# Correlation matmuls joined by four on 32-row groups, and the last head pair's sums on 32 columns, in an eight-image attention and correlation kernel

## The chip, the core and the metric

The kernel runs on one core of a Trainium2 chip. Its engines are TensorE (PE in the profile, its weight loads PEld), VectorE (DVE), ScalarE (ACT), GpSimd (POOL) and SyncE (SP), which issues most of the DMAs. Each engine has a queue of its own and takes its instructions in their order. The metric is the device time of one launch in microseconds (us), lower is better.

## The reference

Input: eight images of 768 channels by 1024 pixels (32 x 32), float32. Two layers follow each other, each behind a group norm and added to its input. Layer 0 is an attention with 12 heads of 64 whose scores are the product of two vectors; layer 1 puts 28 correlations of the image with itself, shifted by up to three pixels, beside the 768 channels and multiplies all 796 by a weight.

```python
# layer 0
qkv = x_flat @ W_qkv.T                                  # 12 heads of 64
var_v = jnp.var(v, axis=-1, ddof=1, keepdims=True)
var_k = jnp.var(k, axis=-1, ddof=1, keepdims=True)
scores = var_v @ jnp.swapaxes(var_k, -2, -1) * scale
out = jax.nn.softmax(scores, axis=-1) @ v
out = out.reshape(B, N, C) @ W_proj.T + b_proj
...
# layer 1
feat_n = feature / jnp.maximum(norm, EPS)
corr = jnp.stack([jnp.sum(feat_pad[:, :, r:h + r, cc:w + cc] * feat_n, axis=1) for r, cc in _offsets()], axis=1)
x = jnp.concatenate([feature, corr], axis=1)            # 768 + 28 channels
out = jnp.einsum('bchw,oc->bohw', x, conv_w) + conv_b[None, :, None, None]
...
x = x + layer0(_gn(x))
x = x + layer1(_gn(x))
```

`_offsets()` are the two diagonals, the middle column and the middle row of a 7 by 7 window.

## The kernel before

**Products.** The large matrix products (keys and values, the projection, the 768-channel part of layer 1, called conv here) go by a fast scheme with 7 products for 8 blocks. The products are numbered 1 to 7; those of one output group g are added up in PSUM tiles named `x`, `y` and `z` (`BANK`, two tiles of x and two of y, which z uses too). `PAIR` and `SINGLE` give the order of (g, p) for the projection and the conv: groups 0 and 1 in turn, then group 2. A product of these two is 12 matmul records in the profile, one for each of three blocks, two column halves and the two passes of float32. `Banks.begin` issues one, `Banks.close` sets when VectorE takes the finished tile (`Wide.take`), and the next product into that tile waits for it. The weights come as tiles `wt`, one for each product, loaded by SP in `t_stream.keys` order as the tiles come free. Sums of operands that the scheme needs (t1, t2, third, t4) are made by VectorE; `t1o` to `t4o` belong to the projection, `t1f` to `t4f` to the conv.

**Attention.** Since the scores of a head are an outer product, `ex` is one ACT instruction with a scale for each row. Two heads make a pair `hp` of six; a pair has eight steps `t`. In each step ACT makes two `ex` tiles and TensorE adds `ex` by `v` into `av` (`Pair.products`, L763, eight records a step). For pairs 3, 4 and 5 (in image 0 for pair 0 too) the denominators are the column sums of `ex`: VectorE adds the eight steps into `acc_5_0` and `acc_5_1` (one tile for each head), and TensorE multiplies them by ones. For the other pairs ACT sums over rows (L748, `junk`) and the inverses go to their places by way of DRAM (`di`, `rd`). `Pair.sum_up` (L797) does it with 32 columns of ones, all four blocks of head and half side by side in one PSUM tile `den`, whose rows go by DRAM to a narrow tile, get their reciprocal there, and come back as `rd`. `Pair.sum_up_last` (L847), for the last pair, uses 64 columns of ones and two PSUM tiles, so that the sums stand on the partitions that need them, and VectorE takes four reciprocals of 128 x 256 into `acc_5_0`. `Pair.finish` multiplies `v` (the pair's output) by the inverses.

**Correlation.** `Corr.gram` (L1101) makes the products of each pixel with those around it, `diagonals` picks the shifted ones, `scale` multiplies by the norm and turns them (`ct`, L340, after `dn`); `gather` (L1174 on, eleven DMAs on SP) puts 40 rows into `cs` (`u`) and `v`, and VectorE multiplies them. 40 channels for 28 correlations: 18 offsets ahead, the same 18 behind, and 4 rows for the middle, with zero weights for those that no correlation uses. `cs` holds three variants of the tokens (first half, second half, difference); rows 0 to 39 are copied to rows 64 to 103.

**Joins.** For images 0 to 6 the correlation part is added inside the conv's own PSUM tiles: 12 products of a conv (p of 2, 3, 7, 4) are left open, and as soon as two are held, `Wide.join` (L1008) adds a matmul with `cs` and `wcorr_sb` to each, the first on rows 0 to 39, the second on rows 64 to 103. The last image's correlation has products and PSUM tiles of its own (L1280).

**Order.** Nothing is scheduled by the tool chain: the program issues instructions in the order in which a model of time (`Clock`) reaches them. `clock.now` follows TensorE, `clock.act` and `clock.dve` follow the two others, `after(us, job)` and `after_dve(us, job)` put a job at a due time, and each job's instructions go to the engine queues in that order. On the chip only the queues and the semaphores count. For each image b + 1 the loop makes keys and values, then `work_off` issues the attention's steps whenever they can run, with the correlation and conv of image b in between. When the rest of that other work is at most `TAIL` us, it is kept back for the gaps and the time after the attention. Then `project(b + 1)` runs the projection, which takes all six pairs' outputs: pairs 0 to 2 in the products of `v` and `t1o`, `t2o` and the later sums with pair 5's too. The projection's results come to `f` (preloaded with the image, `f<-in_x_dram`), on to DRAM as `x1d` and back as the accumulator `x` of the next conv.

At the start TensorE runs `WARM` matmuls on a unit matrix (`warm`, L390) while the first image loads; the group norm's two small products (`pma`, `pva`) follow.

Of the kernel before, what the change touches and what calls it, by code (L numbers as in the profile page):

```python
# [6 lines left out]
F32 = mybir.dt.float32  # L7
# [31 lines left out]
NCH = 2 * NA + 4  # L39
# [11 lines left out]
TAIL = 14.0  # L51
# [3 lines left out]
WARM = 36  # L55
# [13 lines left out]
ORDER = (1, 5, 6, 3, 7, 4, 2)  # L69
OPENING = PAIR[:2] + PAIR[-2:] + PAIR[2:-2]  # L70

# [87 lines left out]
def two_layers(ctx, tc, x, wkv, wproj, bproj, wconv, wcorr, bconv, out):  # L159
# [147 lines left out]
    class TStream:  # L307
        def __init__(self):
            self.keys = []
            for b in range(NB + 1):  # L310
                for kind in ["c"] * (b > 0) + ["p"] * (b < NB):
                    some = PAIR[:-2] if b == NB - 1 and kind == "c" else PAIR
                    self.keys += [(kind, g, p) for g, p in some + SINGLE]
            at = len(self.keys) - len(PAIR + SINGLE)
            self.keys[at:at] = [("c", g, p) for g, p in PAIR[-2:]]
            self.loaded, self.tiles = 0, []
# [25 lines left out]
    class Banks:  # L342
# [11 lines left out]
        def begin(self, g, p, width, pairs, stop=True, between=None):  # L354
            bank = BANK[p]
            of = "x" if bank == "x" else "y"
# [31 lines left out]
    warm = smp.tile([P, 512], F32, tag="sm", name="warm")  # L388
    for n in range(WARM):
        nc.tensor.matmul(warm[:, 0:P], lhsT=ident, rhs=ident, start=True, stop=True)  # L390
# [53 lines left out]
    def load_corr_weights():  # L444
# [5 lines left out]
        for line, step in enumerate(STEP):  # L450
            for j in (1, 2, 3):
                n, k = AHEAD_OF.index(step * j), 3 * line + j - 1
                nc.sync.dma_start(out=wcorr_sb[n : n + 1, :, :], in_=wcorr[k : k + 1, :, :])
                nc.sync.dma_start(out=wcorr_sb[NA + n : NA + n + 1, :, :], in_=wcorr[12 + k : 13 + k, :, :])
        nc.sync.dma_start(out=wcorr_sb[2 * NA : NCH, :, :], in_=wcorr[24:28, :, :])
        nc.sync.dma_start(out=wcorr_sb[HD : HD + NCH, :, :], in_=wcorr_sb[0:NCH, :, :])

# [10 lines left out]
    class Norm:  # L468
# [7 lines left out]
        def means(self):  # L476
            name, mv = self.name, self.mv
            pm = small(f"pm{name}")
            halves(pm[:, 0:1], group_m, mv[:, 0:1])
            self.mean = st.tile([P, 1], F32, tag="mean", bufs=2, name=f"mean{name}")  # L480
# [6 lines left out]
        def spreads(self):  # L487
            name = self.name
            pv = small(f"pv{name}")
            halves(pv[:, 0:1], group_m, self.e)  # L490
            ve = st.tile([P, 1], F32, tag="ve", name=f"ve{name}")
# [216 lines left out]
    class Pair:  # L708
# [80 lines left out]

        def sum_up(self):  # L790
# [3 lines left out]
            for e in range(2):  # L794
                for hf in range(2):
                    at = 2 * e + hf
                    nc.tensor.matmul(  # L797
                        den[at * 32 : (at + 1) * 32, :], lhsT=ones[:, 0:32], rhs=self.acc[e][:, hf * HF : (hf + 1) * HF],
                        start=True, stop=True,
                    )  # L800
# [30 lines left out]
        def load_inverses(self, rows):  # L831
# [5 lines left out]
            self.rd_at = clock.now + (14.0 if (self.b, self.hp) == (1, HP // 2 - 1) else 6.0)  # L837
            self.try_finish()

        def sum_up_last(self):  # L840

            dens = []
            for hf in range(2):
                at = slice(hf * HF, (hf + 1) * HF)
                den = other([P, HF], f"den{self.b}_{self.hp}_{hf}")
                for e in range(2):
                    nc.tensor.matmul(  # L847
                        den[e * HD : (e + 1) * HD, :], lhsT=ones, rhs=self.acc[e][:, at], start=True, stop=True
                    )
                dens.append(den)  # L850
            self.rd = self.acc[0]

            def invert(n):

                q = HF // 2
                vector.reciprocal(self.rd[:, n * q : (n + 1) * q], dens[n // 2][:, n % 2 * q : (n % 2 + 1) * q])
                if n < 3:
                    later.after_dve(1.5 if self.b else 0.0, lambda: invert(n + 1))
                else:
                    self.rd_at = clock.dve  # L860
                    self.try_finish()
# [674 lines left out]
```

## Time and profile before

| what | us |
|---|---|
| runs | 2640.43, 2641.02, 2641.0 |
| median of the runs | 2641.0 |
| profiled execution, its own time | 2640.4 |
| its span, first to last instruction | 2638.7 |
| TensorE busy | 2610.0 |
| VectorE busy | 1604.3 |
| ScalarE busy | 1367.3 |
| GpSimd busy | 413.6 |

The mean granted clock of TensorE is 0.998 of full speed. The DMA queues are busy for some 52% of sixteen engines' time. The span of 2638.7 us lies inside the execution's own time of 2640.4 us; what is left is before the first and after the last instruction.

An image takes some 324 us, most of it one steady pattern that returns in images 2 to 7; image 0 (keys and values of two images, no conv beside) and image 1 differ. In a timeline a line gives the start, the duration from the first start to the modelled last end, the engine, the line of the program, the operation and how many records it stands for; in brackets is idle time just before it and who ended it. Matmuls are pipelined, so the next start tells better than start plus duration when a group is done.

### The profile page before, as it was taken

The page shows a single profiled execution, that of the slowest core. Times are in us where ns is not written, and L with a number is a line of the kernel's source. Part 1 is how long each engine was busy: PE and PEld are TensorE (multiplying, and loading weights), DVE is VectorE, ACT ScalarE, POOL GpSimd, SP SyncE. Part 2 cuts the span into 40 slices and gives each one's busy share as a digit, 9 for nine tenths or more (in the row PEclk, how much of TensorE's full clock was granted, in tenths as well). Part 3 has the DMA queues.
Part 4 walks back from the last instruction along what each step waited for, and adds up shares of the span by engine and source line. Part 5 has one row for each costly group of instructions (what it writes and reads, how often), then busy time and mean ns, then how long its engine had stood idle before and what let it go on. Part 6 is the DMA issues. An engine that isn't in the chain of part 4 may idle for free.

```text
span 2638.7 us, 40466 instructions
## 1 busy us (share of the span) xinstructions
PE 2610.0 (99%) x14766; PEld 1318.2 (50%) x14766; DVE 1604.3 (61%) x4110; ACT 1367.3 (52%) x1841; POOL 413.6 (16%) x444
## 2 busy tenths in 40 slices
PE   9999999999999999999999999999999999999999
PEld 4654566334763347633476334553357433575333
DVE  5858735685447853478534885357853587535864
ACT  1498078711598116980179701897018960199500
POOL 4320130003300033000430003300133001320000
PEclk9999999999999999999999999999999999999999
DMA  7774455455553545626556265562655626545333
GB/s 285 291 247 147 144 198 158 137 182 159 188 187 113 201 153 180 198 95 214 155 172 196 87 220 158 171 205 81 221 172 154 196 84 237 169 137 164 96 117 101
DMA packets 323392, 446.65 MB, mean 169 GB/s; under 512 B 59458, under 2 KB 245170, under 8 KB 323194
## 3 DMA queue, kind: packets, MB, share of 16 engines
q1 hardware_dynamic: 321962, 441.32, 52.0%
q8 instruction: 117, 1.92, 0.3%
q10 hardware_dynamic: 1232, 2.75, 0.3%
q14 instruction: 81, 0.66, 0.1%
HBM read 377.49 MB, written 64.40 MB: 167 GB/s over the span
## 4 chain that ended last, share of the span: by engine, by line
PE 89%; DMA 3%; ACT 3%; DVE 2%; issue 1%; SPq 1%; POOL 1%; DVEq 0%; ACTq 0%; POOLq 0%
PE x L337 35%; PE av L763 22%; PE y L337 17%; PE z L337 9%; PE gr L1101 3%; ACT ex L738 1%; ACT junk L748 1%; DMA x<-x1d 1%; DMA v<-rows 1%; DMA bc<-vdr 1%; PE x L1008 1%; PE den L797 1%; PE y L1008 1%; PE z L1008 1%; DVE acc L153 1%
## 5 line engine op out<-in xcount | busy, mean ns | idle before, releaser
L738 ACT ACTIVATE ex<-bc,nk 128x1024 f32<-128x1024 f32 x768 | 828.2, 1138 | 418.7 <-DMA bc<-vdr 202.6
L763 PE MATMUL av<-ex,v 128*64 128x512 f32 x3072 | 700.2, 596 | 3.4 <-ACT ex L738 3.2
L763 PEld LDWEIGHTS av<-ex,v 128*64 128x64 f32 x3072 | 316.6, 137 | 339.0 <-issue 210.5
L748 ACT ACTIVATE junk<-bk,vm 128x1024 bf16<-128x1024 f32 x368 | 420.5, 1143 | 25.3 <-DMA bk<-kdr 15.5
L153 DVE TENSOR_TENSOR acc<-acc,ex 128x1024 f32<-128x1024 f32 x300 | 344.3, 1209 | 0.0
L215 ACT COPY kp<-x 128x384 f32<-128x384 f32 x28 | 13.4, 477 | 562.1 <-PE x L337 553.4
L337 PE MATMUL y<-kv,s 128*64 128x384 f32 x1488 | 269.4, 487 | 0.0
L337 PE MATMUL x<-kv,xn 128*64 128x384 f32 x1512 | 264.3, 489 | 1.6 <-DVE xn L153 1.6
L337 PE MATMUL x<-kv,s 128*64 128x384 f32 x1488 | 258.2, 486 | 0.0
L337 PEld LDWEIGHTS x<-kv,xn 128*64 128x64 f32 x1512 | 145.3, 138 | 101.1 <-issue 80.5
L337 PEld LDWEIGHTS x<-kv,s 128*64 128x64 f32 x1488 | 145.2, 137 | 91.2 <-issue 67.6
L337 PEld LDWEIGHTS y<-kv,s 128*64 128x64 f32 x1488 | 140.7, 137 | 87.1 <-issue 69.2
L494 POOL TENSOR_TENSOR rstda<-vea,neghalf 128x1 f32<-128x1 f32 x8 | 4.8, 595 | 964.4 <-DVE vea L153 964.4
L1086 POOL TENSOR_TENSOR turn<-f,ones 128x384 f32<-128x384 f32 x112 | 110.9, 1010 | 248.3 <-PE gr L1101 167.6
L337 PE MATMUL z<-kv,xn 128*64 128x384 f32 x768 | 135.1, 486 | 0.0
L337 PE MATMUL x<-v,wt 128*64 128x512 f32 x576 | 131.1, 594 | 0.0
L337 PE MATMUL x<-f,wt 128*64 128x512 f32 x504 | 120.1, 594 | 0.0
L153 DVE TENSOR_TENSOR v<-y,v 128x128 f32<-128x128 f32 x180 | 40.9, 282 | 127.3 <-PE y L337 127.3
L600 POOL TENSOR_TENSOR s<-xn 128x384 f32<-128x384 f32 x64 | 66.8, 1052 | 287.2 <-PE x L337 199.0
L153 DVE BATCH_NORM_STATS2 vbn<-v 128x6 f32<-128x64 f32 x720 | 101.6, 209 | 0.0
L337 PEld LDWEIGHTS z<-kv,xn 128*64 128x64 f32 x768 | 76.4, 137 | 45.9 <-issue 34.3
L1101 PEld LDWEIGHTS gr<-f,turn 128*64 128x64 f32 x1344 | 88.3, 137 | 13.2 <-issue 5.2
(192 smaller groups left out, 3006.5 us busy)
## 6 DMA issues: line engine op xcount, KB each, us to landing
kv<-kvs SPq DMA_DIRECT2D x124, 576.0 KB
kv<-in_wkv_dram SPq DMA_DIRECT2D x95, 576.0 KB
bc<-vdr SPq DMA_DIRECT2D x96, 512.0 KB
f<-in_x_dram SPq DMA_DIRECT2D x48, 512.0 KB
bk<-kdr SPq DMA_DIRECT2D x46, 512.0 KB
x1d<-f SPq DMA_DIRECT2D x42, 512.0 KB
x<-x1d SPq DMA_DIRECT2D x42, 512.0 KB
out_dram<-x SPq DMA_DIRECT2D x82, 256.0 KB
```

Source lines behind the costliest of these rows:

```text
L153: return getattr(self.engine, name)(*args, **kw)
L215: nc.scalar.copy(to, at)
L337: nc.tensor.matmul(out[at], lhsT=lhsT[:, at], rhs=rhs, start=start, stop=stop, **kw)
L494: nc.gpsimd.tensor_tensor(self.rstd, ve, neghalf[:, 0:1], ALU.pow)
L600: nc.gpsimd.tensor_tensor(self.sums[g][:, 0], a[g][2], a[g][3], ALU.add)
L738: nc.scalar.activation(ex, self.bc[e], AF.Exp, scale=self.kv.nk[self.half][:, h, t : t + 1])
L748: nc.scalar.activation(junk, self.bk[e], AF.Exp, scale=self.kv.m2[self.half][:, h, t : t + 1], accum_out=self.sums[:, e, t : t + 1],)
L763: nc.tensor.matmul(self.av[e * HD : (e + 1) * HD, hf, :], lhsT=self.vt[:, t, e, :], rhs=exs[e][:, hf * HF : (hf + 1) * HF], start=t == 0, ...
L797: nc.tensor.matmul(den[at * 32 : (at + 1) * 32, :], lhsT=ones[:, 0:32], rhs=self.acc[e][:, hf * HF : (hf + 1) * HF], start=True, stop=True,)
L1008: nc.tensor.matmul(t, lhsT=wcorr_sb[at, i, :], rhs=cs[at, tokens, :], start=False, stop=True, skip_group_check=True)
L1086: nc.gpsimd.tensor_tensor(to[:, :, side], half, windows(ones, ones.ap[0], (0, J), (HW, 4), (1, HW)), ALU.mult)
L1101: nc.tensor.matmul(ps[side * HD : (side + 1) * HD, :n].rearrange("p (y x) -> p y x", x=WIDE), lhsT=block[:, j, side, :], rhs=image[:, 4 * ...
```

## The change

Five edits, all in the order and form of work; what is computed stays the same.

1. *Channels.* The offsets are listed as four runs of three (`PICKED`), so 12 + 12 + 4 = 28 channels are gathered instead of 40, by 14 DMAs instead of 11. `wcorr_sb` and `cs` are copied to rows 32, 64 and 96 (three copies of 28 rows, before one of 40).
2. *Joins by four.* For the conv of images 0 to 5, a new order (`QUADS`) holds four products, joins them by four matmuls on rows 0, 32, 64 and 96, does that twice, and joins the last four by twos. One product, (0, 2), stands in a tile of the small PSUM pool (`apart`). Image 6 keeps six joins of two, at rows 0 and 32. Per conv: 2 joins of four and 2 of two, before 6 of two.
3. *Last pair's sums.* `sum_up_last` uses the 32-column products of `sum_up` (now `ones_products`), one PSUM tile, two reciprocals of 128 x 256 into `acc_5_1`, and then eight DMAs on SP (32 rows x 512, 64 KB each) which copy each block of rows twice into the 64 partitions of `acc_5_0` that need it. Its reciprocals are due 1.7 us after the products (before 1.2), the copies 0.5 us after the second one.
4. *Less held.* `TAIL` goes from 14 to 11, so that in the order written out av_5's eight steps follow each other in images 2 to 7, with one product with its join between them and `den_5`; before, one product stood between the two halves of av_5. VectorE's order changes with it: in images 2 to 7 the takes of two conv tiles (`x<-z`, `x<-x`) now stand ahead of the reciprocals, and the multiplication of pair 4 (`v*rd`) behind them. `rd_at` of the other pairs goes from 6 to 8 us.
5. *Start and image 0.* 42 warm matmuls instead of 36, in the `av` tile; 6 more behind `pma` and 12 behind `pva` (`BRIDGE`). In image 0 `ct` is issued 5.0 us after its operands' due time instead of 0.7, which puts `ct_0` behind two more steps of av and a `gr`.

```diff
-NCH = 2 * NA + 4
+PICKED = ((1, 1), (31, 1), (62, 2), (93, 3))
+CHANNELS = [first + apart * n for first, apart in PICKED for n in range(3)]
+NS = len(CHANNELS)
+NCH = 2 * NS + 4
...
-TAIL = 14.0
+TAIL = 11.0
...
-WARM = 36
+WARM, BRIDGE = 42, (6, 12)
...
+QUADS = PAIR[:10] + ((0, 2),) + PAIR[10:12] + ((1, 2), (2, 5), (2, 1)) + SINGLE[2:]
+FOUR = P // 4
...
+def conv_order(b):
+    return QUADS if b < NB - 2 else (PAIR[:-2] if b == NB - 2 else PAIR) + SINGLE
...
-        def begin(self, g, p, width, pairs, stop=True, between=None):
+        def begin(self, g, p, width, pairs, stop=True, between=None, apart=False):
             bank = BANK[p]
+            if apart:
+                t = other([P, width], f"{bank}{g}")
+                for k, (lhsT, rhs) in enumerate(pairs):
+                    halves(t, lhsT, rhs, start=k == 0, stop=False, skip_group_check=True)
+                return ("apart", g), t
...
-    warm = smp.tile([P, 512], F32, tag="sm", name="warm")
-    for n in range(WARM):
-        nc.tensor.matmul(warm[:, 0:P], lhsT=ident, rhs=ident, start=True, stop=True)
+    warm = avp.tile([P, 512], F32, tag="av", name="warm")
+    def keep_warm(count):
+        for n in range(count):
+            nc.tensor.matmul(warm[:, 0:P], lhsT=ident, rhs=ident, start=True, stop=True)
+    keep_warm(WARM)
...
-        nc.sync.dma_start(out=wcorr_sb[HD : HD + NCH, :, :], in_=wcorr_sb[0:NCH, :, :])
+        for n in range(1, 4):
+            nc.sync.dma_start(out=wcorr_sb[n * FOUR : n * FOUR + NCH, :, :], in_=wcorr_sb[0:NCH, :, :])
...
             halves(pm[:, 0:1], group_m, mv[:, 0:1])
+            if name == "a0":
+                keep_warm(BRIDGE[0])
...
             halves(pv[:, 0:1], group_m, self.e)
+            if name == "a0":
+                keep_warm(BRIDGE[1])
...
+        def ones_products(self, den):
+            for at in range(4):
+                e, hf = divmod(at, 2)
+                nc.tensor.matmul(
+                    den[at * 32 : (at + 1) * 32, :], lhsT=ones[:, 0:32], rhs=self.acc[e][:, hf * HF : (hf + 1) * HF],
+                    start=True, stop=True,
+                )
...
-            self.rd_at = clock.now + (14.0 if (self.b, self.hp) == (1, HP // 2 - 1) else 6.0)
+            self.rd_at = clock.now + (14.0 if (self.b, self.hp) == (1, HP // 2 - 1) else 8.0)
...
         def sum_up_last(self):
-            dens = []
-            for hf in range(2):
-                at = slice(hf * HF, (hf + 1) * HF)
-                den = other([P, HF], f"den{self.b}_{self.hp}_{hf}")
-                for e in range(2):
-                    nc.tensor.matmul(
-                        den[e * HD : (e + 1) * HD, :], lhsT=ones, rhs=self.acc[e][:, at], start=True, stop=True
-                    )
-                dens.append(den)
-            self.rd = self.acc[0]
+            den = other([P, HF], f"den{self.b}_{self.hp}")
+            self.ones_products(den)
+            self.rd, rc = self.acc[0], self.acc[1][:, 0:HF]
+            q = HF // 2
             def invert(n):
-                q = HF // 2
-                vector.reciprocal(self.rd[:, n * q : (n + 1) * q], dens[n // 2][:, n % 2 * q : (n % 2 + 1) * q])
-                if n < 3:
-                    later.after_dve(1.5 if self.b else 0.0, lambda: invert(n + 1))
-                else:
-                    self.rd_at = clock.dve
-                    self.try_finish()
-            later.after(1.2 if self.b else 0.0, lambda: invert(0))
+                vector.reciprocal(rc[:, n * q : (n + 1) * q], den[:, n * q : (n + 1) * q])
+                later.after_dve(0.5, spread if n else lambda: invert(1))
+            def spread():
+                for at in range(4):
+                    e, hf = divmod(at, 2)
+                    to = self.rd[e * HD : (e + 1) * HD, hf * HF : (hf + 1) * HF]
+                    rows = rc[at * 32 : (at + 1) * 32, :]
+                    for half in range(2):
+                        nc.sync.dma_start(out=to[half * 32 : (half + 1) * 32, :], in_=rows)
+                self.rd_at = clock.now + 5.0
+                self.try_finish()
+            later.after(1.7 if self.b else 1.0, lambda: invert(0))
...
-                self.held.append((*banks.begin(g, p, HF, pairs, stop=False, between=between), taken, *more))
-                if len(self.held) == 2:
+                apart = (g, p) == (0, 2) and self.joined[:1] == [4]
+                self.held.append((*banks.begin(g, p, HF, pairs, stop=False, between=between, apart=apart), taken, *more))
+                if len(self.held) == (self.joined[0] if self.joined else 2):
+                    self.joined = self.joined[1:]
                     self.join()
...
             for n, (slot, t, taken, i, tokens) in enumerate(self.held):
-                at = slice(n * HD, (n + 1) * HD)
+                at = slice(n * FOUR, n * FOUR + NCH)
...
-                later.after_dve(0.7, lambda: to_dram(dn))
+                later.after_dve(0.7 if b else 5.0, lambda: to_dram(dn))
...
-            nc.sync.dma_start(out=u[0:NA, :], in_=r[2:NROW, PAD : PAD + N])
-            nc.sync.dma_start(out=v[NA:NCH, :], in_=windows(r[0:1, PAD:], (0, NA + 4), (1, N)))
...
+            for n, (first, apart) in enumerate(PICKED):
+                k, row = 3 * n, 2 + AHEAD_OF.index(first)
+                nc.sync.dma_start(out=u[k : k + 3, :], in_=windows(r[row : row + 1, PAD:], (apart * ROW, 3), (1, N)))
+                nc.sync.dma_start(out=v[k : k + 3, :], in_=windows(r[0:1, PAD + first :], (apart, 3), (1, N)))
...
-                nc.sync.dma_start(out=cs[HD : HD + NCH, :, :], in_=cs[0:NCH, :, :])
+                for n in range(1, 4):
+                    nc.sync.dma_start(out=cs[n * FOUR : n * FOUR + NCH, :, :], in_=cs[0:NCH, :, :])
...
+            self.wide.joined = [4, 4] if self.b < NB - 2 else []
```

## The prediction

> **What bounds the kernel now.** I read the busy times first. TensorE (PE) works 2610.0 of 2638.7 us; DVE and ACT have 39% and 48% of the span idle. So a microsecond counts only if it leaves TensorE's own queue of work or one of the few gaps in it. The list of what TensorE waited for gives the gaps; its timeline around the change prices each product.
>
> ```profile
> PE 2610.0 (99%) x14766; PEld 1318.2 (50%) x14766; DVE 1604.3 (61%) x4110; ACT 1367.3 (52%) x1841; POOL 413.6 (16%) x444
> ```
> ```profile
> PE x L337 <- DVE x L153: 4.6, 6, 0.9
> PE ct L340 <- DVE dn L153: 3.3, 1, 3.3
> ...
> PE ptv L340 <- DVE vm L153: 2.3, 3, 1.2
> ```
> (total, how often, longest). The timeline of TensorE in image 2 (start, duration, name; the next start, not start plus duration, tells when work is done):
> ```profile
> 800.18 2.74 PE L337 MATMUL y<-f,wt 128*64 128x512 f32 x12
> 802.86 0.69 PE L1008 MATMUL x<-cs,wcorr_sb 64*128 64x512 f32 x1
> 802.86 0.69 PE L1008 MATMUL y<-cs,wcorr_sb 64*128 64x512 f32 x1
> 803.39 0.59 PE L1008 MATMUL x<-cs,wcorr_sb 64*128 64x512 f32 x1
> 803.40 0.59 PE L1008 MATMUL y<-cs,wcorr_sb 64*128 64x512 f32 x1
> 803.91 7.09 PE L763 MATMUL av<-ex,v 128*64 128x512 f32 x32
> ...
> 850.61 1.06 PE L797 MATMUL den<-acc,ones 128*32 128x512 f32 x8
> 851.61 7.09 PE L763 MATMUL av<-ex,v 128*64 128x512 f32 x32
> ...
> 874.27 1.94 PE L847 MATMUL den<-acc,ones 128*64 128x512 f32 x8
> 876.04 2.74 PE L337 MATMUL y<-f,wt 128*64 128x512 f32 x12
> 879.51 2.79 PE L337 MATMUL x<-t4f,wt 128*64 128x512 f32 x12 [0.72 <-DVE x L153]
> ```
> A product of 12 records takes 2.575 us (24 in 893.65 to 898.80). The two correlation matmuls of a join run in pairs on two row groups, 0.53 us a pair, 1.05 in all; with the changes of form before and after (802.755 by the product's rate, 803.91 plus 0.05 that the next av loses) a join costs 1.2.
>
> **The sum, part by part** (us, minus is a gain).
>
> *Joins.* Images 0 to 5 go from six joins of two to two of four and two of two: 12 fewer. If four row groups run together as two do, a four costs no more than a two: -14.4. I add 0.05 for each four's two further starts: **-13.8**. If they ran two by two, a four would take 1.15 + 1.05 = 2.2 and 12 x (2.4 - 2.2) = -2.4 is left. I take the first: the eight records of L797 are four 32-column matmuls and take 1.00 in all, so this array does run four at once in the other direction, and the rows above show two. The four sums stand in four different PSUM tiles. The Trainium skill, "TensorE: Matmul & The Clock Gate", Part 3, Measured speedup, speaks for less: it gives 3.07 times for four row tiles at 512 columns; with a lone matmul as two records of 0.43 us (2.575 / 12, times the two column halves that run together), that estimate puts four at 4 x 0.86 / 3.07 = 1.12, and the part at -13.6. No row here shows four row groups.
>
> *Sums of the last pair.* 64 columns took 1.77 (874.27 to 876.04), 32 columns 1.00: -0.77 in images 2 to 7, -0.57 in image 1, where 545.03 to 546.75 stands less the 1.15 of a den with its change of form: **-5.2**. Both are rows, so the bounds are narrow (-4 to -5.4).
>
> *The wait before x<-t4f.* DVE did one reciprocal (875.43, 1.76) and v*rd (877.10, 1.16) before it freed the x bank at 878.77. In the new order both evacuations stand ahead of the reciprocals. By starts the loss was 879.51 - 878.62 = 0.9, with the weight load 0.95: six times, **-5.7** (0 to -5.7).
>
> *av_5 in one piece.* The product that stood between its halves gave ACT 2.6 us to get ahead with ex. Image 0 had the halves together: 63 records from 246.62 and the last until 261.19, 14.5 against 13.74 for two normal halves. I take +0.8 in images 2 to 7: **+4.8**; ends 0 and +1.4 each (ACT's mean ex of 1138 ns followed by hand over sixteen).
>
> *Reciprocals and the spread.* Four of 1.68 become two, ending 4.9 after the start of den_5 (T0). But eight DMAs must now copy the rows to their partitions, and on SP they stand behind a wt load that waits for x<-t4f to end (T0 + 1.0 + 2 x 2.58 = T0 + 6.2). SP issues small copies at 0.28 each (four den<-ds in 1.13), so they go from T0 + 6.7 to T0 + 9, land at about T0 + 12 (2.1 from di at 814.13 to the dependent rd at 816.26, more for 64 KB), and f<-in_x_dram behind them leaves at T0 + 9.8 instead of coming at 882.97. It lands 5.0 later (887.96 in DVE's timeline), at T0 + 14.8; then f<-x (0.7), v_5 times the inverse (1.2) and the first t2o (0.6): T0 + 17.5. TensorE wants t2o after den, y, x, a join of two and 48 records of v and t1o: 1.0 + 5.15 + 1.2 + 10.3 = T0 + 17.65. It meets with next to nothing over; I charge +0.3 in images 1 to 7: **+2.1** (0 to +3 each).
> ```profile
> 882.97 0.56 SPq L1336 DMA_DIRECT2D f<-in_x_dram  x1
> ```
> ```profile
> 887.96 0.75 DVE L153 SCALAR_TENSOR_TENSOR f<-x,bproj_sb,f 128x512 f32<-128x512 f32 x1 [2.23 <-DMA f<-in_x_dram]
> ```
>
> *Image 0's t2o* waited 1.62 at 288.74; the spread there stands behind a wt that waits for the first t1o product: **+1.5** (0 to +4).
>
> *ct in image 0.* Its 3.3 wait for dn goes, as some 4 us of other work (av, gr) now stands ahead of ct: it runs at about 395.7 as today, so nothing after it is later: **-3.3** (0 if dn slips with it).
>
> *Channels and gather.* 28 rows instead of 40 change no matmul's length: 512 columns move either way. But the gather is 14 DMAs instead of 11, on SP ahead of x<-x1d, and that load is late today:
> ```profile
> 760.90 0.26 SPq L1185 DMA_DIRECT2D v<-rows  x1
> 761.20 0.29 SPq L1186 DMA_DIRECT2D cs<-rows  x1
> 761.59 0.40 SPq L292 DMA_DIRECT2D kv<-in_wkv_dram  x1
> 762.10 0.42 SPq L1214 DMA_DIRECT2D x<-x1d  x1
> ```
> ```profile
> 766.85 0.75 DVE L153 SCALAR_TENSOR_TENSOR x<-x,bconv_sb,x 128x512 f32<-128x512 f32 x1 [3.94 <-DMA x<-x1d]
> ```
> DVE waits for x1d, vm follows, and ptv on TensorE follows vm at once (vm from 769.02, 0.24; ptv at 769.32). Three more issues at 0.39 each (760.41 to 761.59) make x1d 1.17 late. In images 2 to 6 ptv has 0 to 0.3 to spare, in image 7 1.3: 5 x 1.17 less 0.3 = **+5.5** (0 if the late load catches up, +15 if SP waits for one more landing, about 2 us as at 757.94 to 759.93). The two further cs<-cs copies delay nothing that TensorE needs: 20 us lie between 775.82 and the first join at 796.50.
>
> *Start.* After 72 warm records TensorE idles from 12.55 to 16.87 but for pma and pva, and the first 24 real records take 5.79 instead of 3.87, at a granted clock of 0.50 (the third number from the right in the table of stretches):
> ```profile
> 18.00:19.00 1.00, 1.00 (x4) 0.24 (x2) 1.00 (x3) 1.00 (x2) 0.30 (x1) 0.50 1.10 410
> 19.00:20.00 1.00, 1.00 (x6) 0.49 (x4) 1.00 (x2) 1.00 (x3) 1.00 (x1) 0.50 0.11 40
> ```
> The 18 new warm matmuls fill these gaps. If that keeps the clock, 1.9 is won and some 0.6 lost to the mean and spread steps queued behind them: **-1.3** (-1.6 to +0.5).
>
> The sum: -13.8 - 5.2 - 5.7 + 4.8 + 2.1 + 1.5 - 3.3 + 5.5 - 1.3 = **-15.4**. The profiled execution took 2640.4, so 2625.0; the median of the runs, 2641.0, stands 0.6 above it: **2625.6**. All terms at their lower ends give -30; all at their upper ends, joins still four at once, +28.
>
> **Rivals.** (1) *Four row groups run two by two.* For it: only two are seen together. Against: L797. Then -2.4 for -13.8: 2625.6 + 11.4 = 2637.0. (2) *Waits on the middle way take the room*: ptv 2 us late in five images (+10 for +5.5) and av_5 at its upper end (+8.4 for +4.8): 2625.6 + 8.1 = 2633.7. For it: DVE already waits 2.4 to 5.0 us for x1d. Against: SP's later waits are for loads long on their way. (3) *Slower: the spread.* The eight copies and f behind them, on one SP queue, beside xn and wt loads, arrive so late that TensorE waits before x<-t2o in images 1 to 7. The gain is gone from (15.4 + 2.1) / 7 = 2.5 us each, that is if f<-x starts later than T0 + 17.5 instead of T0 + 14.8; at 5 us it is 2625.6 + 7 x 4.7 = 2658.5. For it: the chain reaches t2o with 0.15 to spare, and every step of it is a DMA. Against: a wait of 2.5 needs the copies to take half as long again as the rows say. (4) *No change*: the gains are all cover for something else, 2641. Against: joins and dens are pure work of a 99% busy engine.
>
> **Chances.** Forecast 0.68, (1) 0.10, (2) 0.10, (3) 0.09, (4) 0.03. A measurement of this kernel tells about 0.2% (5.3 us) from no change, so faster means under 2635.7: the forecast, (2) and a little of (1), 0.79; the same, most of (1) and (4), 0.11; slower 0.10. The range, 2612 to 2641, takes in rivals (1) and (2) and leaves out (3) and the lowest corner.
>
> **What would show it.** Four L1035 records with starts within 0.1 us and a whole four-way join near 1.1 (right) or 2 (rival 1). den of the last pair at 1.00. No wait of x<-t4f for DVE x. A wait of av for ACT ex near 0.8 in images 2 to 7. The waits of x<-t2o for DVE t2o and of ptv for DVE vm: 2 and about 8 in total if I am right, over 17 for t2o under rival 3. Clock 1.00 from 17 us on. I am wrong if one of the waits I charge by hand is twice its price, or if the joins take their old time.

## The result, and the profile after

The changed kernel is slower: 2667.9 us median (2664.2 to 2671.1, five runs) against 2641.0 for the kernel before (2640.4 to 2646.2), a ratio of 1.0095 with a 95% interval of 1.0080 to 1.0109. The forecast was 2625.6, with 2612 to 2641 as its range. The profiled execution took 2671.1 us (span 2669.4), 30.8 more than that of before.

TensorE is busy for 2612.1 us, against 2610.0 before, so its work has not grown by 30 us. The page's first line of the changed kernel:

```profile
PE 2612.1 (98%) x14814; PEld 1349.3 (51%) x14814; DVE 1575.2 (59%) x4094; ACT 1366.4 (51%) x1841; POOL 414.5 (16%) x444
```

The list of what TensorE waited for in the changed kernel (total, times, longest) has new or longer entries at the top (ptv for vm stood at 2.3 before, t2o at 1.6):

```profile
PE ptv L349 <- DVE vm L163: 17.3, 5, 4.2
PE x L346 <- DVE t2o L163: 15.6, 7, 6.5
PE x L346 <- DVE x L163: 6.6, 1, 6.6
PE it L349 <- DVE invs L163: 3.3, 1, 3.3
```

All entries of such a list add up to 53.2 us, against 23.8 before. That is 29.4 more. Second, the granted clock: I added up, over all stretches of 1 us, what was missing to full clock. It is 6.1 us before and 23.3 after (0.9 and 1.1 of it behind the last instruction). Losses come in portions of 1.71 us, which is half of some 3.4 us at a clock of 0.50: three such portions before, thirteen after. All but one of the thirteen stand at the new or longer waits; the one at 484 us has its like before, at 478. The table of stretches around the ptv of image 2 in the changed kernel (the third number from the right is the clock; TensorE's busy time comes first after the length):

```profile
782.00:784.00 2.00, 0.69 (x4) 0.00 (x0) 0.00 (x0) 1.97 (x5) 0.00 (x0) 1.00 1.07 401
784.00:786.00 2.00, 0.00 (x0) 0.00 (x0) 1.47 (x6) 2.00 (x3) 0.00 (x0) 0.79 1.04 421
786.00:788.00 2.00, 1.09 (x5) 0.85 (x7) 1.97 (x8) 1.97 (x3) 0.43 (x1) 0.50 1.01 410
788.00:790.00 2.00, 2.00 (x8) 1.04 (x6) 2.00 (x5) 2.00 (x4) 0.00 (x0) 0.50 0.47 193
790.00:792.00 2.00, 2.00 (x7) 1.06 (x5) 2.00 (x10) 1.97 (x4) 0.00 (x0) 0.50 0.05 12
792.00:794.00 2.00, 2.00 (x12) 1.27 (x10) 1.34 (x2) 2.00 (x4) 0.00 (x0) 1.00 0.72 260
```

TensorE stands still for 4.2 us until 786.9, and then works at half clock until 792: 8 and 7 matmul records in two stretches of 2 us, where the next one, at full clock, has 12. Waits (+29.4) and clock (+17.2) make 46.6; the execution grew by 30.8, so some 16 us of work did go, as the change meant; the slower clock hides that in the busy time. (A portion may lie partly in a wait, so this is a bound rather than a sum.)

**The pieces that went as meant.** TensorE's timeline in image 2 of the changed kernel, first a join of four, then the end of the image:

```profile
818.91 2.90 PE L346 MATMUL y<-f,wt 128*64 128x512 f32 x12
821.74 0.69 PE L1035 MATMUL y<-cs,wcorr_sb 28*128 28x512 f32 x1
821.75 0.70 PE L1035 MATMUL x<-cs,wcorr_sb 28*128 28x512 f32 x2
821.76 1.10 PE L1035 MATMUL y<-cs,wcorr_sb 28*128 28x512 f32 x2
...
822.81 2.79 PE L346 MATMUL z<-f,wt 128*64 128x512 f32 x12
825.43 5.32 PE L786 MATMUL av<-ex,v 128*64 128x512 f32 x24
...
893.05 1.07 PE L817 MATMUL den<-acc,ones 128*32 128x512 f32 x8
894.05 2.80 PE L346 MATMUL y<-f,wt 128*64 128x512 f32 x12
896.68 2.75 PE L346 MATMUL x<-t4f,wt 128*64 128x512 f32 x12
```

The first records of all four matmuls start within 0.03 us. The join costs 1.37 us in all: from 821.485 (the start of the product before it, 818.91, plus 2.575) to 822.855 (the product behind it ends at 825.43, so by its rate it began 2.575 earlier). den_5 takes 1.00, and x<-t4f follows y<-f with no wait.

**The pieces that did not.** The same image, SP, then DVE, then TensorE, around the eight spread copies:

```profile
899.46 0.53 SPq L333 DMA_DIRECT2D wt<-tsp  x1
900.04 5.08 SPq L883 DMA_DIRECT2D acc<-acc  x8
905.21 0.53 SPq L1364 DMA_DIRECT2D f<-in_x_dram  x1
```
```profile
909.98 0.75 DVE L163 SCALAR_TENSOR_TENSOR f<-x,bproj_sb,f 128x512 f32<-128x512 f32 x1 [8.13 <-DMA f<-in_x_dram]
910.65 1.22 DVE L163 TENSOR_TENSOR v<-v,acc 128x1024 f32<-128x1024 f32 x1
911.78 1.89 DVE L163 TENSOR_TENSOR t2o<-v,t1o 128x512 f32<-128x512 f32 x3
```
```profile
912.52 5.37 PE L346 MATMUL x<-t2o,wt 128*64 128x512 f32 x24 [1.59 <-DVE t2o L163]
```

SP needs 5.08 us to issue eight copies, 0.64 each. The rest of the chain is nearly as reckoned: the weight load ahead of them goes at 6.4 us after den_5 began (6.2 reckoned), f lands 4.8 us after its issue (5.0). With T0 = 893.05 for den_5's start, f<-x begins at T0 + 16.9, where T0 + 14.8 was reckoned.

The gather, on SP, on DVE and on TensorE (ct first):

```profile
771.79 0.27 SPq L1209 DMA_DIRECT2D cs<-rows  x1
773.49 0.23 SPq L1210 DMA_DIRECT2D v<-rows  x1
776.02 0.23 SPq L1211 DMA_DIRECT2D cs<-rows  x1
...
778.75 0.42 SPq L1239 DMA_DIRECT2D x<-x1d  x1
```
```profile
784.46 0.75 DVE L163 SCALAR_TENSOR_TENSOR x<-x,bconv_sb,x 128x512 f32<-128x512 f32 x1 [7.99 <-DMA x<-x1d]
```
```profile
764.75 2.26 PE L346 MATMUL y<-kv,s 128*64 128x384 f32 x12
766.69 0.43 PE L349 MATMUL ct<-ident,dn 128*64 128x128 f32 x3
...
786.91 0.45 PE L349 MATMUL ptv<-ident,vm 128*48 128x128 f32 x1 [4.21 <-DVE vm L163]
```

In the kernel before, ct stands ahead of that y<-kv of 1.93 us (one of its twelve records runs between those of ct):

```profile
751.18 0.43 PE L340 MATMUL ct<-ident,dn 128*64 128x128 f32 x3
751.56 2.10 PE L337 MATMUL y<-kv,s 128*64 128x384 f32 x11
```

The gather hangs on ct, x1d on the gather, ptv on x1d. TensorE now comes to ptv 1.93 us sooner after ct than it did. From ct to the issue of x1d it is 12.1 us (766.69 to 778.75), 10.9 before (751.18 to 762.10); from there to the take of x 5.7, before 4.8 (762.10 to 766.85).

### The profile page after: what moved, and what is told of

Its sections match the earlier page's. It is cut to its first block, busy times and chain, and to the rows that moved or that the text cites. A ratio compares the mean times of both kernels' runs of the same rounds, so it can differ in the third digit from the quotient of the medians.

```text
span 2669.4 us, 40692 instructions
## 1 busy us (share of the span) xinstructions
PE 2612.1 (98%) x14814; PEld 1349.3 (51%) x14814; DVE 1575.2 (59%) x4094; ACT 1366.4 (51%) x1841; POOL 414.5 (16%) x444
## 3 DMA queue, kind: packets, MB, share of 16 engines
q8 instruction: 118, 1.93, 0.3%
q10 hardware_dynamic: 1232, 2.75, 0.3%
## 4 chain that ended last, share of the span: by engine, by line
PE 89%; DMA 4%; DVE 3%; SPq 2%; issue 1%; ACT 1%; POOL 0%; DVEq 0%; POOLq 0%; ACTq 0%
PE x L346 34%; PE av L786 24%; PE y L346 16%; PE z L346 9%; PE gr L1128 3%; SPq L883 1%; DMA x<-x1d 1%; DVE acc L163 1%; PE den L817 1%; DMA out_dram<-x 1%; PE warm L406 1%; DMA bc<-vdr 1%; DVE v L163 1%; PE z L1035 1%; DMA kv<-kvs 0%
## 5 line engine op out<-in xcount | busy, mean ns | idle before, releaser
L786 PE MATMUL av<-ex,v 128*64 128x512 f32 x3072 | 708.5, 599 | 2.2 <-ACT ex L761 2.2
L786 PEld LDWEIGHTS av<-ex,v 128*64 128x64 f32 x3072 | 333.2, 138 | 326.6 <-issue 203.6
L346 PEld LDWEIGHTS x<-kv,xn 128*64 128x64 f32 x1512 | 138.6, 137 | 104.7 <-issue 88.6
L346 PE MATMUL x<-f,wt 128*64 128x512 f32 x504 | 125.9, 601 | 0.0
L163 DVE SCALAR_TENSOR_TENSOR f<-x,bproj_sb,f 128x512 f32<-128x512 f32 x72 | 53.6, 745 | 75.4 <-DMA f<-in_x_dram 51.6
```

What stands on the lines that cost most here:

```text
L163: return getattr(self.engine, name)(*args, **kw)
L346: nc.tensor.matmul(out[at], lhsT=lhsT[:, at], rhs=rhs, start=start, stop=stop, **kw)
L786: nc.tensor.matmul(self.av[e * HD : (e + 1) * HD, hf, :], lhsT=self.vt[:, t, e, :], rhs=exs[e][:, hf * HF : (hf + 1) * HF], start=t == 0, ...
```

## The experiments

Absolute times differ from chip to chip by some us (the kernel before had medians of 2638.1 to 2641.8 in these sets), so each run stands against the kernel before on its own chip.

| run | median, us | before, us | difference | ratio, 95% interval |
|---|---|---|---|---|
| the change | 2667.9 | 2641.0 | +26.9 | 1.0095 (1.0080 to 1.0109) |
| a_act | 2644.4 | 2638.1 | +6.3 | 1.0021 (1.0010 to 1.0032) |
| a_rd6 | 2670.2 | 2638.1 | +32.1 | 1.0127 (1.0105 to 1.0150) |
| a_join2 | 2684.2 | 2638.1 | +46.1 | 1.0176 (1.0157 to 1.0194) |
| b_gather14 | 2669.8 | 2638.1 | +31.7 | 1.0122 (1.0106 to 1.0138) |
| b_rd8 | 2649.7 | 2641.8 | +8.0 | 1.0032 (1.0021 to 1.0044) |
| b_split | 2645.4 | 2641.8 | +3.7 | 1.0011 (1.0001 to 1.0022) |
| a_fill | 2660.7 | 2641.8 | +19.0 | 1.0066 (1.0045 to 1.0086) |
| best1 | 2648.4 | 2641.8 | +6.7 | 1.0023 (1.0009 to 1.0038) |
| r1 | 2627.5 | 2639.2 | -11.7 | 0.9954 (0.9938 to 0.9969) |
| r1g | 2633.7 | 2639.2 | -5.4 | 0.9980 (0.9971 to 0.9989) |
| r1g_old | 2677.0 | 2639.2 | +37.8 | 1.0144 (1.0131 to 1.0158) |
| r1_t14 | 2629.8 | 2640.9 | -11.1 | 0.9959 (0.9944 to 0.9974) |

Names with a_ start from the changed kernel, with b_ from the kernel before, with r1 from the changed kernel with three corrections.

### The spread copies on another queue (a_act)

```diff
-                        nc.sync.dma_start(out=to[half * 32 : (half + 1) * 32, :], in_=rows)
+                        nc.scalar.dma_start(out=to[half * 32 : (half + 1) * 32, :], in_=rows)
```

> The changed kernel with the eight spread copies issued on ACT's queue instead of SP's; every engine's compute order stays as it is. Theory (it is the issue of eight copies at 0.64 us, behind a weight load, on the queue that f needs): waits of x<-t2o for t2o go from 15.6 to at most 3 us, the wait of x<-v in image 1 from 6.6 to 2 to 4, six or more half-speed windows go, time about 2645. Rival (the copies land late through DMA load, whoever issues them): t2o still waits over 8 us, time over 2658.

The difference to the kernel before fell from 26.9 to 6.3. The compute order of every engine is unchanged, so these 20 us belong to where the copies are issued. TensorE's list of waits:

```profile
PE ptv L349 <- DVE vm L163: 13.9, 5, 3.8
PE x L346 <- DVE x L163: 3.8, 1, 3.8
...
PE x L346 <- DVE t2o L163: 2.1, 2, 1.8
```

t2o went from 15.6 to 2.1, image 1's wait from 6.6 to 3.8, ptv's from 17.3 to 13.9, and the half-speed portions from thirteen to nine (four went, where six or more were expected). ACT takes at least as long for the eight (5.07 us in image 1, 5.68 to 6.00 in the others); but no load that TensorE waits for stands behind them there. The theory holds for t2o; that the copies land late whoever issues them is out, since t2o would still wait over 8 us.

### The place of ct, and the further DMAs, each alone (b_rd8, b_split)

```diff
-            self.rd_at = clock.now + (14.0 if (self.b, self.hp) == (1, HP // 2 - 1) else 6.0)
+            self.rd_at = clock.now + (14.0 if (self.b, self.hp) == (1, HP // 2 - 1) else 8.0)
```

> The kernel before with rd_at of the other pairs at 8 us instead of 6, nothing else. In the order written out the last y<-kv product (1.93 us) then stands ahead of ct_1 in images 2 to 7. Theory (ct one product later makes gather, x1d, vm and ptv that much later against TensorE's queue): ptv's waits grow from 2.3 to some 11 us, with two or three half-speed windows behind them, time 2650 to 2656. Rival (this number is harmless and only the further DMAs count): 2641.

+8.0, with ptv's waits at 8.6 us (2.3 before) and two half-speed portions behind them, somewhat less than forecast. One number in the model of time, meant for a multiplication on DVE, moves ct past a product on TensorE: by the code, ct is due a set time after DVE's modelled work, and that work now ends later, so the product comes out first. In images 2 to 7 its place is the only difference in TensorE's order (in image 0 `it` passes a few records of a product); in VectorE's, the multiplications by rd and some steps of the next image's group norm move too, so that the 8.0 need not be ct's alone.

```diff
-            nc.sync.dma_start(out=u[0:NA, :], in_=r[2:NROW, PAD : PAD + N])
+            nc.sync.dma_start(out=u[0:9, :], in_=r[2:11, PAD : PAD + N])
+            nc.sync.dma_start(out=u[9:NA, :], in_=r[11:NROW, PAD : PAD + N])
...
```

The 22 rows of v and the 4 rows of u are cut in two in the same way.

> The kernel before with its three largest gather DMAs each cut in two, so 14 instead of 11, none overlapping another. Theory (each issue costs x1d some 0.4 us): ptv's waits grow from 2.3 to about 7 us, time 2645 to 2650. Rival (taken up by what follows): ptv waits under 4 us, 2641.

ptv's waits came to 8.5 us, the time to +3.7 (0.3 to 5.8 by its interval). So three more issues cost 6.2 us of waiting over five images (1.24 each; 1.17 was forecast), and ct's place 6.3. Together they are 12.5 of the 15.0 by which ptv's waits grew; another 3.4 went in a_act, so they hung on the copies in SP's queue. The three need not add up exactly, as no run has them in pairs.

### A later x1d by itself (b_gather14)

```diff
+            for n in range(3):
+                nc.sync.dma_start(out=u[2 * NA : NCH, :], in_=windows(r[1:2, PAD:], (0, 4), (1, N)))
```

> The kernel before with three more small gather DMAs (the middle four rows loaded four times instead of once), nothing else. Theory (each issue delays x1d, which ptv waits for): ptv's waits grow from 2.3 to about 8 us, time 2646 to 2650. Rival (the delay is taken up by the loads that follow): time 2641.

A miss that taught something: these three write the same rows, and issuing them took 3.9 us, 1.3 each where the others take about 0.3; I read it so that each waited on SP for the one before it to land. The run says nothing of a count of DMAs, but it prices lateness: ptv's waits rose by 15.7 to 18.0 us, all waits by 18.3 (23.8 to 42.1), the clock's loss by ten to 16.0, and the time of the profiled execution, 2665.5, stands 27.4 above the median of the kernel before (the median of this kernel 31.7). So 18.3 us of waiting cost about one and a half times their length.

### Matmuls in the wait (a_fill)

```diff
         pt = small(f"pt{name}")
+        if name in [f"v{b}_1" for b in range(2, 7)]:
+            for n in range(12):
+                nc.tensor.matmul(pt[:, 0:P], lhsT=ident, rhs=ident, start=True, stop=True)
```

> The changed kernel with 12 matmuls of 128 columns on the unit matrix (2.9 us at full clock) ahead of the ptv that waits in images 2 to 6; their result is overwritten. Theory (a wait of 2 to 4 us brings a window of 3.4 us at half speed, and that costs as much again): the half-speed windows behind ptv go, 4 to 6 of 13, and though no wait gets shorter the time falls to about 2660. Rival (the low clock costs nothing beside the wait, or isn't caused by it): 2664 to 2674.

The difference fell from 26.9 to 19.0 with not one dependency changed. All five portions behind ptv are gone (the clock's loss falls from 23.3 to 13.1), and the vm chain is not earlier on the whole: from ct to ptv the five images take 97.4 us together, 97.2 in the changed kernel, single ones up to 1.5 more or less. Image 2 in this kernel:

```profile
783.29 2.94 PE L579 MATMUL ptv<-ident 128*128 128x128 f32 x24
786.17 0.31 PE L349 MATMUL ptv<-ident,vm 128*48 128x128 f32 x1
...
787.95 2.93 PE L346 MATMUL x<-f,wt 128*64 128x512 f32 x12
790.53 2.93 PE L346 MATMUL y<-t1f,wt 128*64 128x512 f32 x12
```

x<-f takes 2.58 us here (787.95 to 790.53). So the low clock behind ptv comes from the standstill. It costs about 8 us of the 26.9 (five portions of 1.71 are 8.6); by the intervals of the two ratios the gain is 1 to 14 us.

### rd_at back for all pairs (a_rd6)

```diff
-            self.rd_at = clock.now + (14.0 if (self.b, self.hp) == (1, HP // 2 - 1) else 8.0)
+            self.rd_at = clock.now + (14.0 if (self.b, self.hp) == (1, HP // 2 - 1) else 6.0)
```

> The changed kernel with rd_at of the other pairs back at 6 us. In the order written out this puts ct_1 of images 2 to 7 ahead of the last y<-kv product (1.93 us) again, where it stood before the change. Theory (ct's place and the gather's three further DMAs make x1d, vm and ptv late): the waits of ptv for vm go from 17.3 to about 8 us in total, most of the clock windows behind them go too, time about 2653. Rival (the gather's DMAs or their landing alone make ptv late): ptv still waits 14 us or more, time 2664 to 2671.

ptv's waits fell to 6.7, as the theory had it, but the time did not fall. The same number also puts the multiplication of pair 4 between the two reciprocals, and the spread then stands on SP behind f, a weight load and two out_dram: t2o waits 23.4 instead of 15.6, and f, late now too, another 4.6 before other products. The waits add up to 53.7 us, as before this edit (53.2): they moved on.

### Joins by two (a_join2)

```diff
-    return QUADS if b < NB - 2 else (PAIR[:-2] if b == NB - 2 else PAIR) + SINGLE
+    return PAIR + SINGLE if b < NB - 2 else (PAIR[:-2] if b == NB - 2 else PAIR) + SINGLE
...
-            self.wide.joined = [4, 4] if self.b < NB - 2 else []
```

> The changed kernel with all joins by two in the old order of products, 28 channels at rows 0 and 32. Theory (a join of four costs 1.37 us against 2.4 for two joins of two, so that the change won 12 x 1.03 there): TensorE's busy time and the time rise by about 12, to 2680, if the waits stay. Rival (joins of four give nothing in the whole): 2668 or less.

TensorE's busy time rose by 11.8 us (2623.9 against 2612.1), which is 12 times 0.98; the reading 12 times 1.03 off the timeline fits. The difference to the kernel before rose by 19, and t2o waits 30.1 us in this run, where the order of products moved as well. Joins by four pay what one reads off them.

### Everything taken back at once, too much of it (best1)

Here rd_at is 6, the spread is on ACT's queue, image 1's multiplication is due 4 us later (next run), and the gather comes 14 us after its rows instead of 3 (the product of its rows 11 us after it instead of 18).

> The changed kernel with what the runs so far blame taken back: rd_at 6 us, spread copies on ACT's queue and the multiplication with them in image 1 due 4 us later, gather of images 1 on due after the first loads of x1d instead of ahead of them. Theory (joins of four, 32-column sums and the order of the takes are worth about 20 us, the waits ate them): ptv waits under 2 us, t2o under 3, time 2618 to 2628. Rival (a further cost is hidden in the change): over 2636.

+6.7, another miss. ptv waits no more, but the copies cs<-cs and di, rd for the inverses of pair 2 stand on SP behind the moved gather, and DVE stood 13.3 us before one multiplication, with a take of a conv tile behind it:

```profile
793.46 1.23 DVE L163 TENSOR_TENSOR v<-v,rd 128x1024 f32<-128x1024 f32 x1 [13.29 <-DMA rd<-di]
794.60 0.74 DVE L163 SCALAR_TENSOR_TENSOR x<-x,bconv_sb,x 128x512 f32<-128x512 f32 x1
```

TensorE waits 9.0 us for such takes in six images, 8.3 for t2o and 5.5 for f.

### Three small corrections (r1)

```diff
-            self.rd_at = clock.now + (14.0 if (self.b, self.hp) == (1, HP // 2 - 1) else 8.0)
+            self.rd_at = clock.now + (14.0 if (self.b, self.hp) == (1, HP // 2 - 1) else 6.0 if self.hp < 1 else 8.0)
...
-                        nc.sync.dma_start(out=to[half * 32 : (half + 1) * 32, :], in_=rows)
-                self.rd_at = clock.now + 5.0
+                        nc.scalar.dma_start(out=to[half * 32 : (half + 1) * 32, :], in_=rows)
+                self.rd_at = clock.now + (9.0 if self.b == 1 else 5.0)
```

The third needs image 1's DVE order in the changed kernel to be understood. There, the multiplication with the spread inverses (v<-v,acc) stands ahead of two takes, the last two lines:

```profile
559.18 0.68 DVE L163 TENSOR_TENSOR x<-x,x 128x512 f32<-128x512 f32 x1
569.88 1.22 DVE L163 TENSOR_TENSOR v<-v,acc 128x1024 f32<-128x1024 f32 x1 [10.02 <-DMA acc<-acc]
571.03 1.89 DVE L163 TENSOR_TENSOR t1o<-v 128x512 f32<-128x512 f32 x3
572.83 0.68 DVE L163 TENSOR_TENSOR x<-y,x 128x512 f32<-128x512 f32 x1
573.43 0.74 DVE L163 SCALAR_TENSOR_TENSOR x<-x,bconv_sb,x 128x512 f32<-128x512 f32 x1
```

DVE stands for 10 us waiting for the copies, and TensorE's next product, which needs the bank that the last line frees, waits 6.6 us. In the kernel before, the takes came first:

```profile
560.13 0.74 DVE L153 SCALAR_TENSOR_TENSOR x<-x,bconv_sb,x 128x512 f32<-128x512 f32 x1
560.78 1.22 DVE L153 TENSOR_TENSOR v<-v,acc 128x1024 f32<-128x1024 f32 x1
```

> The changed kernel with three corrections: spread copies on ACT's queue, in image 1 the multiplication with them due 4 us later, and rd_at 6 us for pair 0 alone, which puts ct_1 back ahead of the last y<-kv product and leaves every other order of images 2 to 7. Theory: against the run with ACT's queue alone the waits of ptv fall from 13.9 to 5 to 8 us, that of x<-v in image 1 from 3.8 to under 1, half-speed windows from 8 to about 4, time 2628 to 2634. Rival (the waits move on to another place as in the kernel with rd_at 6 for all): over 2640.

0.9954: faster than the kernel before by 11.7 us. In the profile ptv waits 5.1 us, x<-v in image 1 does not wait at all, t2o only in image 0 (3.0), and there are four half-speed portions (nine in a_act). This is the best version of this study, with 0.9938 to 0.9969 as its interval.

### The gather ahead of the kv loads (r1g)

```diff
-                    later.after(3.0, self.gather)
+                    later.after(3.0 if b == 0 else 0.3, self.gather)
```

> The kernel with the three corrections, and the gather of images 1 on due 0.3 us after its rows instead of 3, so that its 14 DMAs stand ahead of two kv loads on SP instead of behind them. Theory (the 7th and 8th gather DMA wait on SP for those 576 KB loads to land): the gather loses its two pauses of 1.7 and 2.5 us, x1d comes about 2 us earlier, ptv waits under 2 us in total, time 2620 to 2628. Rival (the copies of the gather wait for their rows as long): ptv as in the kernel without this, same time within 3 us.

In this run the product of the gathered rows is also due 20.7 us after the gather instead of 18, so that it keeps its time. Missed: six us slower than r1. The pauses inside the gather went, as the theory had it, but the gather now waits for its own rows to land first (2.2 us after their last issue), so x1d is issued 8.9 us after the rows in both kernels (752.48 to 761.42, and 751.62 to 760.59). And the two kv loads now go just ahead of x1d, and ptv waits 11.9 us instead of 5.1; that they are why was not tested apart.

### The old sums in the new order (r1g_old)

```diff
-            den = other([P, HF], f"den{self.b}_{self.hp}")
-            self.ones_products(den)
...
+                vector.reciprocal(self.rd[:, n * q : (n + 1) * q], dens[n // 2][:, n % 2 * q : (n % 2 + 1) * q])
+                if n < 3:
+                    later.after_dve(1.5 if self.b else 0.0, lambda: invert(n + 1))
```

sum_up_last is that of the kernel before: 64 columns, two tiles, four reciprocals, no copies.

> The kernel with corrections and the early gather, but with the last pair's sums as before the change: 64 columns, two PSUM tiles, four reciprocals, no spread. Theory (the sums by 32 columns win 0.77 us an image on TensorE and, off SP, cost nothing): 5 us slower than with them, more if x<-t2o waits for the two reciprocals more. Rival (the spread costs as much as the columns save): the same within 2 us or faster.

43 us slower than r1g: the rival is out, and of the theory only its "more if" came. In this order the fourth reciprocal stands on DVE behind a take f<-x that waits for the projection's first products (5.9 us in image 2), and t2o waits 31.7 us over seven images. So the run says little about the price of 64 columns, and much about due times: the order is only right for the sums that it was made for.

### Less held, undone (r1_t14)

```diff
-TAIL = 11.0
+TAIL = 14.0
```

> The kernel with the three corrections and TAIL back at 14. av_5 stays in one piece in images 2 to 7; there one product z<-f moves from before den_4 to behind av_5, and in image 0 two kv products move behind av_5 and den_5 ahead of three others. Theory (holding less is worth next to nothing by itself; image 0 lost its wait for t2o and two half-speed windows by it): 0.3 to 0.5% faster than the kernel before less some 4 us, that is a ratio of 0.993 to 0.996. Rival (less held is what frees x<-t4f): its waits for x come back, six of about 0.9, ratio 0.997 or above.

0.9959, the same as r1 within the intervals. With the other edits in place av_5 is in one piece either way. Image 0 gains (t2o waits 0.7 there, and only one half-speed portion is left in the whole run), images 2 to 7 lose it again (f 5.5 and x 2.1 us of waits, small and in every image). Holding less is worth nothing by itself here.

## Why the prediction was wrong, step by step

- *Joins:* right in kind, four row groups do run at once; a four costs 1.37 rather than 1.25, so -12.4 for the forecast -13.8 (11.8 in a_join2). The four matmuls themselves take 1.07 (821.74 to 822.81). What I lacked lies ahead of them: the first starts 0.26 us after the product's end by rate, 0.11 in a join of two. The estimate from the 3.07 times of the Trainium skill ("TensorE: Matmul & The Clock Gate", Part 3, Measured speedup vs the span model) was 1.12 for the four, close to the row's 1.07, which decides.
- *Sums of the last pair:* right: 1.00 for 1.77.
- *The wait before x<-t4f:* right, it is gone.
- *av_5 in one piece:* forecast +0.8 an image, and 1.0 measured in image 2 (874.55 to 889.3, by what follows, against 13.74).
- *ct in image 0:* right, the wait is 0.4 instead of 3.3. But some 78 us further on, in image 1, TensorE now waits 3.3 for invs and 1.9 for ex (482.91 and 485.23), where it waited 2.45 for ex before (477.70). No term has these 2.75 us more, and no run tests whether ct's gain was lost again there.
- *Start:* -1.3 forecast, nothing measured. The clock stayed at 1.00, so that the first 24 records run in 3.92 us, but they start at 18.60 instead of 16.87 behind the new warm matmuls: the second group starts at 22.52 (22.49 before). The 1.9 to be won was also read too high: 5.79 runs to the last end, 3.87 from start to start; from start to start the slow group took 5.62 (16.87 to 22.49). Nor do the new warm matmuls always keep the clock: of the ten traces with this start one, a_fill, has a portion at 14 to 19 us.
- *Reciprocals and the spread:* the step that failed in size. "SP issues small copies at 0.28 each (four den<-ds in 1.13)" took the price of a copy of one row for one of 32 rows. It is 0.64, so that the eight took 2.8 us more than the 2.3 reckoned. The chain that met "with next to nothing over" was so 2.1 us late in image 2 (f<-x at T0 + 16.9 for T0 + 14.8): 0.9 to 2.7 us of waiting in each of images 2 to 7, 9.1 in all where +2.1 had been charged (image 1's share with it), and 6.5 instead of some 3.1 in image 0. a_act shows what the copies cost in SP's queue, all waits and half-speed portions that go with them taken together: 20.6 us. The slower rival (3) named the mechanism, but with a threshold of 2.5 us an image, more than came in all but one (2.67 at 2221); it was one of three causes.
- *Image 1:* failed in place. I charged +0.3 as in the images after it, but in the changed kernel its DVE order differs: the multiplication with the copies stands ahead of the takes that free a bank. 6.6 us of waiting, and two half-speed portions behind it.
- *Gather:* +5.5 forecast; ptv's waits grew by 15.0. The DMAs were priced well (6.2 in b_split). What failed is that I took "ptv in images 2 to 6 has 0 to 0.3 to spare" as before and did not see ct move past a product by rd_at (6.3 in b_rd8); and the copies on SP made ptv 3.4 later still (a_act). ct's move was in the written-out order of TensorE, and could have been read there.
- *No term at all* for the clock after a wait. The trace before shows it at three places (a portion at 17, 396 and 478 us), and I used only the first, for the start. Ten more portions cost up to 17 us; a_fill gets back about 8 of these without any wait removed.
- *The range:* the terms at their upper ends add up to +31, not +28, and the result, +26.9, lies near that corner: three of them came at or above their upper ends at once (ptv's waits, t2o's in image 0, and the spread's share in image 1). The range stopped at 2641, which is no change, and left that corner out.

Each against the kernel before on its own chip, r1 stands 38.6 us better than the change (26.9 + 11.7): 20.6 by the queue alone (a_act, 26.9 to 6.3), and 18.0 by the two other corrections together with the half-speed portions behind those waits; these two were not run apart. The gain that is then left, 11.7, compares with 15.4 forecast, so of the 42.3 us between forecast and result these causes hold all but 3.7.

## What to carry to other kernels

Price a DMA's issue by a row of its own shape (eight copies of 32 rows took 5.08 us where the price of single rows gave 2.3), since everything behind them on that queue pays. When an order is written out by a model of time, compare the order of every engine before and after, instruction by instruction, for each number that is changed; a due time that moves a multiplication on one engine moved a matmul past its neighbour on another. And where an engine has a clock that falls after a standstill, charge a wait of 2 us or more with what can follow it: here 1.71 us a portion, and up to three portions a wait.

## What the runs showed of the hardware that was not expected

- A standstill of TensorE of 2 us or more can bring 3.4 us at half clock, a loss of 1.71 us a portion, and waits of 4.2 and 6.5 us in the changed kernel brought two and three portions. Whether it comes depends on more than the length: 2.14 us (den, image 0) and 2.67 (t2o at 2221) brought it there, 2.60 (ptv at 1114) and all single waits up to 1.8 us did not. In other runs the spread is wider: 2.01 us (ptv at 2075 in a_act) brought it, 3.89 (ptv at 1762 in b_gather14) did not.
- Issuing a copy of 32 rows of 2 KB within the chip takes SP 0.63 to 0.64 us in the changed kernel (0.73 in image 6), and ACT 0.63 in image 1 of a_act, 0.71 to 0.75 in its other images and up to 1.07 in best1 (image 6). Issuing a copy of one row takes 0.28.
- Four matmuls on four row groups of 28 rows start within 0.03 us of each other and take 1.07 us (821.74 to 822.81); two take 1.05 (802.86 to 803.91 in the kernel before).
